# A four-layer graph transformer on one core: norm by groups between the keys, routed results kept by partition, and the output copied within DRAM

## The chip, the core and the metric

One core of one Trainium2 chip runs the whole network in one launch. The metric is the device time in microseconds (us) of an execution. The core has a matrix engine (TensorE, PE), a vector engine (VectorE, DVE), an engine for activations (ScalarE, ACT), a general engine (GpSimd, POOL) and a queue engine (SyncE, SP). SP, ACT and POOL each issue DMAs; 16 DMA engines carry them out.

## What is computed

3125 nodes with 256 features each pass through four layers. Every layer adds a graph attention over 103,125 edges and a global mixing of the normalised features to `x`, and then a feed-forward part:

```python
xn = _layernorm(x, axis=-1)
x = x + _L1_gnn_ref(xn, ..., src, dst) + _L1_mix_ref(xn[None], ...)[0]
x = x + _L1_ffn_ref(_layernorm(x, axis=-1)[None], ...)[0]
```

The mixing of layers 1 and 2 is linear attention: keys and values of all nodes are multiplied into one 32x32 matrix per head, then every query is multiplied with it. The feed-forward parts of layers 0 and 3 are routed: a softmax over eight experts picks two experts per node in layer 0 and one in layer 3, and the expert's result is weighted by its probability. In layer 3:

```python
H = gelu(xf @ W1 + b1); probs = softmax(H @ Wg + bg); assign = argmax(probs)
out = out + where(assign == e, probs[:, e:e+1] * (H @ Wd[e] + bd[e]), 0.0)   # for each e
```

## The kernel before

All node data stay on chip in tiles of 125 nodes, 25 of them: `x` and `xn` are 125 partitions x 25 x 256, and `xT` is the transposed norm. `GROUPS` cuts the 25 tiles into seven groups of 4, 4, 4, 4, 3, 3, 3. `begin_layer` norms all groups (`layernorm`: statistics on DVE, root on ACT, `xn` on DVE) and transposes them on PE (`transposed`). Most instructions are placed on their engine by a scheduler; inside a `manual_schedule` PE and DVE keep the written order. Work that can fill gaps is a Python generator, advanced by `next(work)`.

The stages, in the order of time:

- Layer 0: counts of edges, global mixing, graph attention with dense tiles, then `routed0`. Its results are scattered by an indirect DMA to `y_d` in DRAM, node by node, in two halves for the two experts; `route` works out which row each place is sent to. At the end both halves are read back in groups as (t p) f, one 1 KB piece per node, by SP (into `xn`) and ACT (into `xT`), and DVE adds them to `x`, weighted.
- Layer 1: `begin_layer`, then `beside`, which starts the generator `node_pieces` (graph attention's products per node tile, in tiles of 128 nodes) and lets `mix1` advance it. `mix1` calls `keys_values`: for each tile a product `p_kvt`, the key by ACT and DVE, the value by ACT, and the sum `p_kv`. Then come queries (`message`) and `network`, which adds `xn` and the bias `b2` to `x` on POOL. After that dense attention, a second attention (`dense_one`), and `ffn1`.
- Layer 2: `begin_layer`, the same with `mix2`, whose first instruction is the addition of `bproj` to all of `x` on POOL. Then dense attention and `ffn2`.
- Layer 3: `edge_attention` runs over the edges in 101 steps of 8 columns. In each, POOL gathers 8 x 128 rows `z_edge` by indirect DMA, DVE and ACT weight them (`near_e`), and PE sums them (`p_acc`). Once all tiles of a group are summed, the generator `hidden3` of that group runs piece by piece between the steps: norm, transposes, product with W1 (`p_h`, 8 parts of 128), Gelu on ACT, the router's scores, softmax, `first_max`, and rows of the hidden layer written to `hid_d` in DRAM through the tile `hid_row` (two buffers). `share` holds each node's probability.
- `routed3`: eight loads of `w_d`, alternately on ACT and SP, one of `bd`, `route`, and then for 32 tiles of 128 places a gather of `hid_tile` from `hid_d`, eight transposes (`p_t`), the product with the chosen expert (`p_q`), the bias, and a scatter to `y_d`. At the end, groups of `y_own` are read from `y_d`, multiplied by `share`, added to `x` and stored:

```python
y = w.tile([TP, 4, C], F32, name="y_own", bufs=4)
(nc.scalar if i % 2 else nc.sync).dma_start(y[:, :nt, :], y_d[t0 * TP:(t0 + nt) * TP, :].rearrange("(t p) f -> p t f", p=TP))
...
(nc.sync if i % 2 else nc.scalar).dma_start(out[:, t0:t0 + nt, :], x[:, t0:t0 + nt, :])
```

Of the kernel before, what the change touches and what calls it, by code (L numbers as in the profile page):

```python
# [42 lines left out]
PIECES0 = 101  # L43
# [3 lines left out]

GROUPS = [(0, 4), (4, 4), (8, 4), (12, 4), (16, 3), (19, 3), (22, 3)]
# [6 lines left out]
class Net:  # L55
# [811 lines left out]
    def keys_values(self, c, w, xT, wkv, work):  # L867
# [4 lines left out]
        with tc.tile_pool(name="la1", bufs=1, space=PSUM) as ps1, tc.tile_pool(name="la4", bufs=5, space=PSUM) as ps:  # L872
            p_kv = [ps1.tile([P, P + 1], F32, name=f"p_kv{m}") for m in range(KC)]
            for t in range(NT):
                ts = slice(t * TP, (t + 1) * TP)
# [9 lines left out]
                next(work, None)  # L885
# [23 lines left out]
    def mix1(self, x, xn, xT, work=iter(())):  # L909
        nc, tc = self.nc, self.tc  # L910
        with ExitStack() as s:
            c = s.enter_context(tc.tile_pool(name="m1", bufs=1))
            wkv = c.tile([P, KC, 2 * C], F32, name="wkv")
            for i, n in enumerate("kv"):
                nc.sync.dma_start(wkv[:, :, i * C:(i + 1) * C], self.ins["L1_mix_W" + n].rearrange("(k p) f -> p k f", p=P))
# [12 lines left out]
            with tc.tile_pool(name="m1k", bufs=2) as wk:  # L928
                kv, den = self.keys_values(c, wk, xT, wkv, work)
# [15 lines left out]
            def network(t0, nt):  # L945
# [24 lines left out]
                nc.gpsimd.tensor_add(xs, xs, xn[:, t0:t0 + nt, :])  # L970
                nc.gpsimd.tensor_add(xs, xs, b2[:, None, :].to_broadcast([TP, nt, C]))
# [108 lines left out]
    def mix2(self, x, xT, work=iter(())):  # L1080
        nc, tc = self.nc, self.tc
        with ExitStack() as s:
# [9 lines left out]

            nc.gpsimd.tensor_add(x, x, bproj[:, None, :].to_broadcast([TP, NT, C]))
            kv, den = self.keys_values(c, w, xT, wkv, work)
# [86 lines left out]
    def mix3(self, w, ps, x, xn, xT, weights):  # L1181
# [7 lines left out]
        zero = w.tile([P, 512], F32, name="hid_row", bufs=2)[:1, :KC * (P + 1)]  # L1189
# [3 lines left out]
        for t0, nt in GROUPS:  # L1193
# [9 lines left out]
            sq = w.tile([P, 8, 512], F32, name="h")[:TP, :2, :].rearrange("p a (b c) -> p (a b) c", c=C)[:, :nt, :]  # L1203
# [16 lines left out]
        s = w.tile([P, 512], F32, name="hid_row", bufs=2)[:, :KC * (P + 1)].rearrange("p (m f) -> p m f", m=KC)  # L1220
        nc.vector.tensor_copy(s, p_kv)
        yield
        kv = w.tile([P, 512], F32, name="hid_row", bufs=2)[:, :C].rearrange("p (m f) -> p m f", m=KC)
# [83 lines left out]
class Dense(Net):  # L1307
# [284 lines left out]
    def node_pieces(self, nodes, name, xT, H, slope, w, ps):  # L1592


        nc = self.nc
# [4 lines left out]
        yield  # L1600
# [7 lines left out]
        yield  # L1608
        es = w.tile([P, NS, H], F32, name="es")
        nc.gpsimd.memset(es[:, NS - 1, :], 0.0)  # L1610
        nc.gpsimd.memset(zs[:, NS - 1, :], 0.0)
# [412 lines left out]
    def route(self, c, one, nj):  # L2024

        nc, tc = self.nc, self.tc  # L2030
        _, T, E = one.shape
        node = c.tile([P, nj], I32, name="node_of")
# [547 lines left out]
```

## Time and profile before

| what | value |
|---|---|
| median of 10 runs | 5737.75 us (5728.58 to 5747.85) |
| profiled execution, and its span | 5742.5 us, 5740.6 us |
| mean granted clock of PE | 0.921 |
| edge attention of layer 3 | about 4400 to 5470 us of the span |
| from there to the first product of `routed3` | 5470 to 5540 us |
| products of `routed3` | 5540 to 5682 us |
| output | 5682 to 5741 us |

The profile is one execution, taken on the chip. PE is TensorE's products, PEld its loading of weights, which overlaps them. A line like "L709 PE MATMUL p_q<-w_d,hid_t" is one group of instructions: line of the code, engine, operation, what is written from what, then shapes, count, busy time and mean duration in ns, and what ended the idle time before it. L709 is the line of the helper `mm`, which issues nearly all products, so groups are told apart by their tiles. Line numbers in the prediction are those of the kernel before.

### The profile page before, as it was taken

What the parts mean: (1) busy time and instruction counts of PE and PEld (TensorE: products, weight loads), DVE (VectorE), ACT (ScalarE), POOL (GpSimd) and SP (SyncE); (2) the same over time, 40 slices, a digit from 0 to 9 for tenths busy, and PEclk for the clock granted to TensorE, in tenths of its full rate; (3) what the DMA queues carried; (4) which work ended last, traced back from release to release, by engine and by line L of the source; (5) the groups of instructions that cost most, each with busy time, mean ns of one, the idle gap of its engine ahead of it and who ended that gap; (6) DMA issues with size and microseconds to landing.
All of it is one profiled execution on the core that took longest, in us unless ns stands there. A gap on an engine that the chain in (4) does not pass through costs nothing.

```text
span 5740.6 us, 66349 instructions
## 1 busy us (share of the span) xinstructions
PE 4921.9 (86%) x24784; PEld 2863.3 (50%) x24784; DVE 3757.2 (65%) x5968; ACT 1022.6 (18%) x1932; POOL 1066.1 (19%) x1195
## 2 busy tenths in 40 slices
PE   3977888879578899989999899979997888898865
PEld 1652234448544433368645433345565555555555
DVE  6779999975445599845443899932223887777722
ACT  1540010011022200110123000022332112232210
POOL 1000000004220000000001100000002777777722
PEclk7989999979889999999889899989998889999978
DMA  2452222232200011111000011110002665666643
GB/s 84 34 38 87 76 64 66 67 113 64 88 16 0 23 34 35 33 42 36 22 1 4 26 33 39 30 58 1 0 1 79 155 159 158 178 171 169 168 157 123
DMA packets 299086, 391.54 MB, mean 68 GB/s; under 512 B 118746, under 2 KB 235583, under 8 KB 298249
## 3 DMA queue, kind: packets, MB, share of 16 engines
q1 hardware_dynamic: 204752, 160.01, 11.8%
q0 software_dynamic: 52336, 162.38, 10.7%
q10 hardware_dynamic: 41670, 64.82, 3.4%
q8 instruction: 202, 3.31, 0.3%
q14 instruction: 126, 1.03, 0.1%
HBM read 340.93 MB, written 46.13 MB: 67 GB/s over the span
## 4 chain that ended last, share of the span: by engine, by line
PE 39%; DVE 6%; DMA 5%; POOL 3%; issue 2%; ACT 1%; SPq 0%; DVEq 0%; ACTq 0%; POOLq 0%
PE p_tr L709 8%; PE p_acc L1976 5%; PE acc L1804 5%; PE p_y L709 5%; PE acc L1753 4%; POOL z_edge L1908 3%; DMA z_edge<-tab,src_i 2%; PE acc L1758 2%; PE p_h L709 2%; PE p_q L709 2%; DVE z_edge L1967 1%; DVE pt L1653 1%; PE p_kvt L709 1%; DVE zinv L1090 1%; DMA y_own<-y_d 1%
## 5 line engine op out<-in xcount | busy, mean ns | idle before, releaser
L1653 DVE SCALAR_TENSOR_TENSOR pt<-q_head,bar,a 128x750 f32<-128x750 f32 (+5 forms) x1200 | 1483.6, 1300 | 77.9 <-PE acc L1758 57.1
L1908 POOL DMA_INDIRECT z_edge<-tab,src_i x806 | 776.0, 963 | 271.9 <-issue 209.6
L1702 PE MATMUL acc<-pt,zs 128*64 128x500 f32 (+2 forms) x2800 | 594.0, 551 | 145.8 <-DVE pt L1653 145.4
L1753 PE MATMUL acc<-pt,zs 128*64 128x375 f32 (+2 forms) x3200 | 605.5, 501 | 18.3 <-DVE pt L1653 18.0
L1976 PE MATMUL p_acc<-z_edge,oh 128*125 128x264 f32 x2044 | 544.5, 428 | 88.6 <-DVE z_edge L1967 88.6
L1976 PEld LDWEIGHTS p_acc<-z_edge,oh 128*125 128x125 f32 x2044 | 423.8, 211 | 194.5 <-DVE z_edge L1967 98.2
L1702 PEld LDWEIGHTS acc<-pt,zs 128*64 128x64 f32 (+1 forms) x2800 | 246.0, 137 | 478.0 <-DVE pt L1653 321.7
L1753 PEld LDWEIGHTS acc<-pt,zs 128*64 128x64 f32 (+1 forms) x3200 | 243.5, 136 | 357.0 <-issue 217.3
L1171 DVE SCALAR_TENSOR_TENSOR x<-p_y,sm,x 125x256 f32<-125x256 f32 x200 | 93.9, 484 | 427.9 <-PE p_y L709 427.9
L1758 PE MATMUL acc<-pt,zs 128*32 128x375 f32 (+2 forms) x3200 | 313.4, 497 | 0.0
L1804 PE MATMUL acc<-zs,pt 128*125 128x257 f32 x1250 | 275.2, 383 | 11.9 <-DMA a<-count_d 11.9
L1804 PEld LDWEIGHTS acc<-zs,pt 128*125 128x125 f32 x1250 | 234.4, 188 | 52.7 <-issue 14.7
L1967 DVE TENSOR_TENSOR z_edge<-z_edge,near_e 128x2112 f32<-128x2112 f32 (+1 forms) x101 | 236.5, 2342 | 18.9 <-ACT near_e L1959 18.9
L1166 ACT ACTIVATE h<-p_tr,bn 128x500 f32<-128x500 f32 (+1 forms) x224 | 161.6, 722 | 361.9 <-PE p_tr L709 361.9
L286 PE MATMUL p_tr<-ident,xn 125*128 125x125 f32 x350 | 71.0, 355 | 165.0 <-DVE xn L612 138.3
L709 PE MATMUL p_y<-w_L_ffn_Wo,h 128*125 128x256 f32 x800 | 203.7, 387 | 0.0
L1653 DVE SCALAR_TENSOR_TENSOR pt<-q_all,bar,a 128x500 f32<-128x500 f32 (+3 forms) x175 | 119.1, 683 | 122.4 <-PE acc L1804 119.8
L709 PE MATMUL p_tr<-h,w_L_ffn_W 128*128 128x500 f32 (+1 forms) x448 | 192.1, 552 | 6.4 <-ACT h L1166 3.2
L1610 POOL MEMSET es<- 128x4 f32 (+2 forms) x4 | 1.3, 334 | 1050.0 <-PE acc L1758 721.3
L709 PE MATMUL p_tr<-xT,w_L_ffn_W 128*128 128x500 f32 (+1 forms) x448 | 194.8, 558 | 0.0
L2281 POOL CAST one_e<-one 125x96 bf16<-125x96 f32 (+1 forms) x2 | 2.1, 1050 | 1029.6 <-PE acc L1702 645.8
L1758 PEld LDWEIGHTS acc<-pt,zs 128*32 128x32 f32 (+1 forms) x3200 | 85.0, 109 | 202.8 <-issue 201.5
(496 smaller groups left out, 7093.1 us busy)
## 6 DMA issues: line engine op xcount, KB each, us to landing
row<-dst_row SPq DMA_DIRECT2D x101, 250.0 KB
a<-count_d SPq DMA_DIRECT2D x96, 203.1 KB
a<-count_d SPq DMA_DIRECT2D x96, 187.5 KB
a<-count_d SPq DMA_DIRECT2D x144, 93.8 KB
ef<-in_edge_s SPq DMA_DIRECT2D x101, 128.0 KB
z_edge<-tab,src_i POOLq DMA_INDIRECT x806
hid_d<-hid_row ACTq DMA_DIRECT2D x50, 250.0 KB
count_d<-stage SPq DMA_DIRECT2D x12, 781.2 KB
```

Source lines behind the costliest of these rows:

```text
L286: nc.tensor.transpose(p[:, t, :], src[:, t0 + t, k * P:(k + 1) * P], self.ident[:TP, :TP])
L709: self.nc.tensor.matmul(p, a, b, start=(i == 0), stop=(i == len(pairs) - 1))
L1166: nc.scalar.activation(o[:, m, :n], p[:, :n], AF.Relu, bias=b[:, e, m:m + 1], scale=g[:, e, m:m + 1])
L1171: nc.vector.scalar_tensor_tensor(x[:, t0 + t, :], q, wf[:, t, e:e + 1], x[:, t0 + t, :], op0=OP.mult, op1=OP.add)
L1653: self.nc.vector.scalar_tensor_tensor(pt[:K, :n], q, bar, a[:K, :n], op0=OP.max, op1=OP.mult)
L1702: nc.tensor.matmul(acc[64 * i:64 * i + 64, :b1 - b0], zs[:K, t, z:z + 64], pts[i][:K, b0:b1], start=(t == 0), stop=(t == NS - 1))
L1753: nc.tensor.matmul(acc[i // 2][64 * (i % 2):64 * (i % 2) + 64, b, :b1 - b0], zs[:K, t, i * W:i * W + 64], pts[i][:K, b0:b1], **st)
L1758: nc.tensor.matmul(acc[2][32 * i:32 * i + 32, b, :b1 - b0], zs[:K, t, z:z + 32], pts[i][:K, b0:b1], **st)
L1804: nc.tensor.matmul(acc[i], pt[:K, i * TP:(i + 1) * TP], zs[:K, t, :C + 1], start=(t == 0), stop=(t == NS - 1))
L1908: nc.gpsimd.indirect_dma_start(out=zs[i][:, j, :], out_offset=None, in_=table, in_offset=bass.IndirectOffsetOnAxis(ap=src[:, c0 + j:c0 + j ...
L1967: nc.vector.tensor_mul(zh, zh, weight[:, :, :, None].to_broadcast([P, n, H, D + 1]))
L1976: nc.tensor.matmul(acc[t], ohs[i, t][:, k - a, :], zs[i][:, k - c0, :HW], start=(k == cols[t][0]), stop=(k == cols[t][1] - 1))
```

## The change

- `begin_layer` before layers 1 and 2 goes. `keys_values` norms two groups first, then transposes each group when its first tile is due and norms the group after the next one. `node_pieces` works group by group and yields how many tiles of `xT` its next piece needs; `keys_values` advances it only when that many are there. `network` adds `xn` and `b2` on DVE, not on POOL. In `mix2` the addition of `bproj` stands after `keys_values`. `wkv` of layer 1 is loaded by POOL's queue.
- Layer 0's routed results and `xn_d` are stored by partition, (p t) f, so that a group's read is one piece of up to 4 KB for each partition; `route` computes the places accordingly.
- Layer 3: `hidden3` runs over `ENDS`, seven groups of three tiles and two of two. A row of `hid_d` has 1281 elements: the hidden row, the share and the node's `x`, which SP's queue writes straight from `x`. `hid_row` has four buffers. In `routed3` the gather brings all three, DVE finishes the row in its tile (share times result plus `x`) before the scatter, SP loads all of `w_d`, and the output is two copies from `y_d` to `out` within DRAM, on SP and ACT.

The diff, cut to its core:

```diff
@@ -40,11 +40,13 @@
 KEYS = HI * GN
-PIECES0 = 101
+PIECES0 = 107
 ...
 MARGIN = 4
+HID = 1024
+ENDS = [(0, 3), (3, 3), (6, 3), (9, 3), (12, 3), (15, 3), (18, 3), (21, 2), (23, 2)]
@@ -864,14 +866,26 @@
-    def keys_values(self, c, w, xT, wkv, work):
+    def keys_values(self, c, w, x, xn, xT, wkv, work):
 ...
         den = c.tile([P, KC, P], F32, name="kden")
-        with tc.tile_pool(name="la1", bufs=1, space=PSUM) as ps1, tc.tile_pool(name="la4", bufs=5, space=PSUM) as ps:
+        with tc.tile_pool(name="la1", bufs=1, space=PSUM) as ps1, tc.tile_pool(name="la4", bufs=3, space=PSUM) as ps, \
+                tc.tile_pool(name="lat", bufs=2, space=PSUM) as pst:
             p_kv = [ps1.tile([P, P + 1], F32, name=f"p_kv{m}") for m in range(KC)]
+            self.layernorm(xn, x, GROUPS[0])
+            self.layernorm(xn, x, GROUPS[1])
+            need, done = 0, 0
+            begins = {g[0]: i for i, g in enumerate(GROUPS)}
             for t in range(NT):
+                if t in begins:
+                    i = begins[t]
+                    self.transposed(pst, xT, xn, groups=[GROUPS[i]])
+                    done = sum(GROUPS[i])
+                    if 0 < i < len(GROUPS) - 1:
+                        self.layernorm(xn, x, GROUPS[i + 1])
@@ -882,7 +896,8 @@
                     nc.tensor.matmul(p_kv[m], key[:, m * P:(m + 1) * P], v[:, m, :], start=(t == 0), stop=(t == NT - 1))
-                next(work, None)
+                if t > 1 and need <= min(done, NT):
+                    need = next(work, 0)
@@ -912,7 +927,7 @@
             for i, n in enumerate("kv"):
-                nc.sync.dma_start(wkv[:, :, i * C:(i + 1) * C], self.ins["L1_mix_W" + n].rearrange("(k p) f -> p k f", p=P))
+                nc.gpsimd.dma_start(wkv[:, :, i * C:(i + 1) * C], self.ins["L1_mix_W" + n].rearrange("(k p) f -> p k f", p=P))
@@ -967,8 +982,8 @@
                 nc.vector.tensor_mul(o, o, g2[:, None, :].to_broadcast([TP, nt, C]))
-                nc.gpsimd.tensor_add(xs, xs, xn[:, t0:t0 + nt, :])
-                nc.gpsimd.tensor_add(xs, xs, b2[:, None, :].to_broadcast([TP, nt, C]))
+                nc.vector.tensor_add(xs, xs, xn[:, t0:t0 + nt, :])
+                nc.vector.tensor_add(xs, xs, b2[:, None, :].to_broadcast([TP, nt, C]))
@@ -1090,8 +1105,8 @@
                 nc.vector.tensor_mul(out, num, z)
+            kv, den = self.keys_values(c, w, x, xn, xT, wkv, work)
             nc.gpsimd.tensor_add(x, x, bproj[:, None, :].to_broadcast([TP, NT, C]))
-            kv, den = self.keys_values(c, w, xT, wkv, work)
@@ -1592,12 +1607,18 @@
         gw = self.gnn_weight(w, ps, name, H, "p_a")
-        yield
+        es = w.tile([P, NS, H], F32, name="es")
 ...
+        yield GROUPS[0][1]
+        at = 0
@@ -1605,19 +1626,16 @@
             nc.sync.dma_start(q_d[:, cs], q)
-        yield
-        es = w.tile([P, NS, H], F32, name="es")
 ...
-        for t in range(NS):
 ...
-            yield
+            yield t0 + nt
+            while at < NS and min((at + 1) * P, N) <= (t0 + nt) * TP:
+                t, at = at, at + 1
 ...
+                yield t0 + nt + (4 if at < NS and min((at + 1) * P, N) > (t0 + nt) * TP else 0)
@@ -1986,7 +2003,7 @@
                         nc.vector.tensor_add(x[:, t, :], x[:, t, :], o.rearrange("p h d -> p (h d)"))
-                        for t0, nt in GROUPS:
+                        for t0, nt in ENDS:
@@ -2048,7 +2066,7 @@
             spare = w.tile([P, nj], F32, name="spare")
-            nc.gpsimd.iota(spare, pattern=[[P, nj]], base=T * TP + 1, channel_multiplier=1, allow_small_or_imprecise_dtypes=True)
+            nc.gpsimd.iota(spare, pattern=[[P, nj]], base=T * TP + (T == NT), channel_multiplier=1, allow_small_or_imprecise_dtypes=True)
@@ -2109,17 +2127,22 @@
             code = w.tile([P, nj], F32, name="code")
-            nc.vector.scalar_tensor_tensor(code, p_n[:, 1], float(TP), n_1, op0=OP.mult, op1=OP.add)
             at_n = w.tile([P, nj], F32, name="at_n")
-            nc.vector.tensor_scalar(at_n, code, -1.0, 0.0, op0=OP.add, op1=OP.max)
             if T > NT:
+                nc.vector.scalar_tensor_tensor(code, n_1, float(NT), p_n[:, 1], op0=OP.mult, op1=OP.add)
+                nc.vector.tensor_scalar(at_n, code, -float(NT), 0.0, op0=OP.add, op1=OP.max)
                 over_n = w.tile([P, nj], F32, name="over_n")
-                nc.vector.tensor_scalar(over_n, at_n, float(N), -float(N), op0=OP.is_ge, op1=OP.mult)
-                nc.vector.tensor_add(node, at_n, over_n)
+                nc.vector.tensor_scalar(over_n, p_n[:, 1], float(NT), float(NT), op0=OP.is_ge, op1=OP.mult)
+                nc.vector.tensor_sub(node, at_n, over_n)
+                nc.vector.scalar_tensor_tensor(at_n, over_n, float(N // NT - 1), at_n, op0=OP.mult, op1=OP.add)
+                nc.vector.scalar_tensor_tensor(spare, code, 0.0, spare, op0=OP.is_equal, op1=OP.mult)
+                nc.vector.tensor_add(to, at_n, spare)
 ...
@@ -2153,15 +2177,16 @@
             yield
-        h = w.tile([P, F, 512], F32, name="h")
+        h = w.tile([P, F, 3 * TP], F32, name="h")
 ...
             nc.scalar.activation(h[:, f, :n], p[:, :n], AF.Gelu, bias=b1[:, f:f + 1], scale=1.0)
-            yield
+            if f % 2:
+                yield
 ...
         self.mm(p[:E, :n], [(wg[:, f, :], h[:, f, :n]) for f in range(F)])
-        sc = w.tile([P, 512], F32, name="hid_row", bufs=2)[:E]
+        sc = w.tile([P, 513], F32, name="hid_row", bufs=4)[:E]
@@ -2173,39 +2198,44 @@
         nc.vector.tensor_mul(one, one, prob)
-        nc.vector.tensor_reduce(share[:, t0:t0 + nt], one, AX.X, OP.add)
+        share = w.tile([TP, 4], F32, name="share")
+        nc.vector.tensor_reduce(share[:, :nt], one, AX.X, OP.add)
+        nc.sync.dma_start(hid_d[t0 * TP:(t0 + nt) * TP, HID + 1:].rearrange("(t p) f -> p t f", p=TP), x[:, t0:t0 + nt, :])
 ...
                     nc.tensor.transpose(p[:TP, f * P:(f + 1) * P], h[:, 4 * i + f, t * TP:(t + 1) * TP], self.ident)
-                row = w.tile([P, 512], F32, name="hid_row", bufs=2)[:TP]
-                nc.scalar.activation(row, p[:TP], AF.Copy)
-                nc.scalar.dma_start(hid_d[(t0 + t) * TP:(t0 + t + 1) * TP, i * 512:(i + 1) * 512], row)
+                row = w.tile([P, 513], F32, name="hid_row", bufs=4)[:TP]
+                nc.scalar.activation(row[:, :512], p[:TP], AF.Copy)
+                if i:
+                    nc.scalar.activation(row[:, 512:], share[:, t:t + 1], AF.Copy)
+                nc.scalar.dma_start(hid_d[(t0 + t) * TP:(t0 + t + 1) * TP, i * 512:(i + 1) * 512 + i], row[:, :512 + i])
                 yield
-    def routed3(self, x, ones, share, hid_d, out):
+    def routed3(self, ones, hid_d, out):
         nc, tc = self.nc, self.tc
-        E, F, HID = 8, 8, 1024
+        E, F = 8, 8
 ...
             for e in range(E):
-                (nc.sync if e % 2 else nc.scalar).dma_start(wd[:, :, e, :], self.ins["L3_ffn_Wd"][e].rearrange("(k p) f -> p k f", p=P))
+                nc.sync.dma_start(wd[:, :, e, :], self.ins["L3_ffn_Wd"][e].rearrange("(k p) f -> p k f", p=P))
 ...
             ps = s.enter_context(tc.tile_pool(name="r3q", bufs=2, space=PSUM))
-            mat, hts = {}, {}
+            mat, hts, hrs = {}, {}, {}
             def rows(j):
-                hr = w.tile([P, HID], F32, name="hid_tile")
+                hr = hrs[j] = w.tile([P, HID + 1 + C], F32, name="hid_tile", bufs=4)
@@ -2224,6 +2254,7 @@
                 nc.vector.tensor_add(y, q, bd[:, bass.ds(mat[j], C)])
+                nc.vector.scalar_tensor_tensor(y, y, hrs[j][:, HID:HID + 1], hrs[j][:, HID + 1:], op0=OP.mult, op1=OP.add)
@@ -2232,13 +2263,10 @@
                         products(j - 1)
-            for i, (t0, nt) in enumerate(GROUPS):
-                y = w.tile([TP, 4, C], F32, name="y_own", bufs=4)
-                (nc.scalar if i % 2 else nc.sync).dma_start(y[:, :nt, :], y_d[t0 * TP:(t0 + nt) * TP, :].rearrange("(t p) f -> p t f", p=TP))
-                for t in range(nt):
-                    nc.vector.scalar_tensor_tensor(x[:, t0 + t, :], y[:, t, :], share[:, t0 + t:t0 + t + 1], x[:, t0 + t, :],
-                                                   op0=OP.mult, op1=OP.add)
-                (nc.sync if i % 2 else nc.scalar).dma_start(out[:, t0:t0 + nt, :], x[:, t0:t0 + nt, :])
+            for i, q in enumerate((nc.sync, nc.scalar)):
+                a, b = i * 62 * 25, 62 * 25 if i == 0 else N
+                q.dma_start(out[a:b, :].rearrange("(p t) f -> p (t f)", t=25), y_d[a:b, :].rearrange("(p t) f -> p (t f)", t=25))
@@ -2264,7 +2292,7 @@
                     self.layernorm_twice(xn, x, (a, na))
-                    nc.sync.dma_start(xn_d[a * TP:(a + na) * TP, :].rearrange("(t p) f -> p t f", p=TP), xn[:, a:a + na, :])
+                    nc.sync.dma_start(xn_d.rearrange("(p t) f -> p t f", p=TP)[:, a:a + na, :], xn[:, a:a + na, :])
@@ -2367,8 +2395,8 @@
                 for i, y in enumerate((xn[:, t0:t0 + nt, :], back)):
-                    a = i * N + t0 * TP
-                    (nc.scalar if i else nc.sync).dma_start(y, y_d[a:a + nt * TP, :].rearrange("(t p) f -> p t f", p=TP))
+                    own = y_d[i * N:(i + 1) * N, :].rearrange("(p t) f -> p t f", p=TP)
+                    (nc.scalar if i else nc.sync).dma_start(y, own[:, t0:t0 + nt, :])
@@ -2416,7 +2444,6 @@
                 self.routed0(x, xn, xT, xn_d, gate, self.routed0_weights(wp))
-        self.begin_layer(x, xn, xT)
@@ -2427,16 +2454,14 @@
             self.ffn1(x, xn, xT, weights)
-        self.begin_layer(x, xn, xT)
 ...
             gw = self.gnn2_weights(ap)
-            nodes = self.beside(ap, "g2", xT, 4, 0.2, lambda work: self.mix2(x, xT, work))
+            nodes = self.beside(ap, "g2", xT, 4, 0.2, lambda work: self.mix2(x, xn, xT, work))
 ...
             ones = lp.tile([TP, NT, 8], BF16, name="one_e")
-            share = lp.tile([TP, NT], F32, name="share")
-            hid_d = self.dram.tile([N, 1024], F32, name="hid_d")
+            hid_d = self.dram.tile([N, HID + 1 + C], F32, name="hid_d")
@@ -2447,8 +2472,8 @@
                     x, xT, edge, lambda w, ps: self.mix3(w, ps, x, xn, xT, mix),
-                    lambda w, ps, t0, nt: self.hidden3(w, ps, x, xn, xT, t0, nt, hid, ones, share, hid_d))
-            self.routed3(x, ones, share, hid_d, out)
+                    lambda w, ps, t0, nt: self.hidden3(w, ps, x, xn, xT, t0, nt, hid, ones, hid_d))
+            self.routed3(ones, hid_d, out)
```

## The prediction

> **What bounds the kernel now.** I read the page first, then a table of stages made from windows of the span, then the chain of waits in the tail, and last the transfer rates, the groups and the timeline of the stages that the change touches. The page says that TensorE (PE) is busy for most of the span and carries most of the chain that ended last. It cannot say which stages leave it idle, and that is what the change is about.
>
> ```profile
> PE 4921.9 (86%) x24784; PEld 2863.3 (50%) x24784; DVE 3757.2 (65%) x5968; ACT 1022.6 (18%) x1932; POOL 1066.1 (19%) x1195
> PE 39%; DVE 6%; DMA 5%; POOL 3%; issue 2%; ACT 1%; SPq 0%; DVEq 0%; ACTq 0%; POOLq 0%
> ```
>
> The table of stages (window, its length, busy time and count of PE, weight loads, DVE, ACT and POOL, then granted clock, DMA share, GB/s) has four stretches in which PE is nearly idle or waits: 1521 to 1588 (read-back after layer 0's routed part), 1588 to 1628 (norm before layer 1), 5497 to 5540 (before the last products) and 5682 to the end.
>
> ```profile
> 1521.00:1588.00 67.00, 0.00 (x0) 0.00 (x0) 20.30 (x50) 1.28 (x1) 0.97 (x3) 0.51 0.46 145
> 1588.00:1628.00 40.00, 13.97 (x53) 9.64 (x54) 38.24 (x90) 5.66 (x14) 30.83 (x18) 0.50 0.02 6
> 1628.00:1720.00 92.00, 91.58 (x333) 51.02 (x333) 15.44 (x54) 36.44 (x107) 2.24 (x22) 0.98 0.01 1
> 3048.00:3056.00 8.00, 7.32 (x50) 6.85 (x50) 6.09 (x15) 3.77 (x8) 5.06 (x2) 0.79 0.14 49
> 3056.00:3152.00 96.00, 91.46 (x334) 50.65 (x335) 19.55 (x53) 36.44 (x107) 11.66 (x25) 0.98 0.00 1
> ...
> 5497.00:5540.00 43.00, 11.18 (x59) 9.35 (x57) 12.15 (x49) 3.58 (x6) 4.06 (x5) 0.50 0.81 284
> 5540.00:5682.00 142.00, 138.74 (x752) 123.24 (x752) 34.63 (x63) 17.95 (x30) 58.57 (x60) 0.99 0.44 138
> 5682.00:5741.00 59.00, 0.00 (x0) 0.00 (x0) 10.34 (x25) 0.00 (x0) 0.00 (x0) 0.52 0.31 109
> ```
>
> The chain of waits (start, length, what) shows what the tail waits for: rows of `hid_d` written twice in a row, then a load, a gather, the products, and the reading of `y_d`.
>
> ```profile
> 5475.14 17.40 PE p_h L709 x48
> ...
> 5496.93 13.04 DMA hid_d<-hid_row
> 5510.68 10.93 DMA hid_d<-hid_row
> 5523.06 7.07 DMA m_L_ffn_bd<-in_L_ffn_bd
> 5530.12 5.11 DMA hid_tile<-hid_d,node_of
> 5535.64 3.91 PE p_t L2215 x16
> 5540.41 5.41 PE p_q L709 x16
> ...
> 5682.88 19.89 DMA y_own<-y_d
> ```
>
> Two strips of GB/s in 40 slices: 5680 to 5741, where everything moves in rows of 125 partitions, and 5497 to 5535, where the 128-partition weights `w_d` move first.
>
> ```profile
> GB/s 38 59 32 97 121 121 121 121 121 121 121 121 121 121 121 121 121 121 120 121 121 121 121 121 120 121 121 121 120 121 124 111 120 121 119 115 121 107 24 0
> GB/s 382 380 384 385 323 356 381 390 392 389 390 388 391 384 389 386 264 355 388 301 128 123 125 125 126 119 122 120 213 315 391 413 397 398 215 161 181 241 362 319
> ```
>
> A 125-row transfer holds 121 GB/s at a DMA share of about 0.3 (the last stage's row), which is five of 16 engines at 24 GB/s each; the weights get 390 from all 16.
>
> **Part 1, output.** Removed: seven loads of `y_own`, 25 DVE multiply-adds and seven stores, which are 6.4 MB at 121 GB/s = 53 us of the 58 from 5682.3 (the last scatter's landing) to the end. Added: one multiply-add per tile on DVE ahead of the scatter (0.48 us, the row of the same operation in the final stage). The products repeat every 4.33 us with PE busy 138.7 of 142, while DVE does 34.6 of 142 and would do 50: hidden on all tiles but the last, so +0.5. The gather's row grows from 4096 to 5124 bytes: 656 KB in 4.33 us is 152 GB/s, below 390, hidden by the prefetch of four tiles; if that cover were gone, a 5.1 us gather instead of 4.33 would cost 0.8 on 32 tiles, 25 us. Then two copies within DRAM, in 32 rows each, 3.2 MB. No such copy is in the trace. At best it moves like the weights, 3.2 MB / 390 = 8.2 us; if reading and writing the same memory halve that rate, 16.4; on five engines, 26.5. Both ends of it are DRAM, unlike the row of the weights, so I take 16.4. With 0.5, 0.6 us to start (5682.3 to 5682.9), a landing of 2.4 (the last scatter's) and about 2 from the last bytes to the end of the span, the stage is 22 and the gain **36** (26 to 45). The Trainium skill, "DMA: Bandwidth & Descriptors", section "Latency and other measured facts", gives copies between HBM tensors a full rate of 207 to 214 GB/s per direction. No run here shows that yet; as an estimate from that page, 3.2 / 0.21 = 15 us, where the weights' row alone would give 8.
>
> **Part 2, the last group.** The last group has two tiles of nodes instead of three. Its `p_h` products, 17.4 us for 375 columns, become 17.4 x 250/375 = 11.6: 5.8 earlier. `hid_row` has four buffers for two: the last group needs one for the scores and four for rows, so the waits of 13.0 and 10.9 us for a buffer mostly go. What is late next is the transfers: 8.4 MB of `w_d`, all on SP's queue behind the last write of `x` rows, which only needs the finished rows; 1 MB of `bd` and 1 MB of rows on ACT's. In before the weights start at 5493.9, just after the last read of `bg` (5493.6); with 5.8 less, 5488. 10.4 MB / 390 = 27 us: 5515 at the latest if the rows share evenly, then gather 5.1, transposes and first product 5.3 (5530.1 to 5540.4 in the chain): 5525, or 5520 if the rows land ahead of the weights. Against 5540.4 I take **18** (8 to 28; the low end is rows that wait behind all of `w_d`). The routing's own DVE work, 12.2 us in the stage's row, is done before that.
>
> **Part 3, edge attention, where the other groups are finished.** Nine groups for seven, the same columns, pieces of two products. The built order has 78 activation table loads between the first and the last `near_e` where before has 74, at 1.28 us each, beside an ACT engine that is mostly idle. Writing `x` beside the rows adds 3.2 MB of 125-row transfers, 26 us of five engines over 1070 us. On the other side, ACT waited 35.5 us for `hid_row`. POOL sets the pace: 806 gathers at 0.96 us and 0.26 of issue between them are 982 of 1070 us. I take **0** (25 either way, from those two figures).
>
> **Part 4, norm by groups in layer 1.** In this stage DVE is the bound, and slowed:
>
> ```profile
> L612 DVE TENSOR_SCALAR xn<-x,mv,rstd 125x256 f32<-125x256 f32 x25 | 24.1, 1025 | 0.0
> L970 POOL TENSOR_TENSOR x<-x,xn 125x1024 f32<-125x1024 f32 (+1 forms) x7 | 14.9, 2128 | 8.2 <-DVE xn L612 8.2
> ```
>
> `xn` takes 1.03 us on average beside POOL's additions, while its median is 0.41. After the change two groups (8 tiles) come first: 8 x (0.40 + 0.16 + 0.41) and 0.8 for the roots is 8.5, eight transposes at 0.43 and a copy of 0.6 are 4: keys start at 1600.5 instead of 1628.3, 27.8 saved. Back come the other 42 transposes on a PE that is full there (91.6 of 92): 42 x 7.32/50 = 6. DVE gets 17 more norms (16.4), 14 additions that were POOL's (the nearest row, a 125x1024 product of two tensors, is 1.08: 13.5 in all), nine keys at 0.42 and the copies of `xT`: some 37 us that the built order puts before the tenth key, against 9 x 3.7 = 33 of PE. I charge 5 for it. POOL no longer works beside DVE, so I keep 0.41 for `xn`. The pieces of the node products go on later, in about the same amount. `wkv` moves to POOL's queue, behind nothing but small fills. Net **17** (3 to 25).
>
> **Part 5, the small ones.** Layer 0's read-back keeps 125 rows and so five engines; only its pieces grow from 1 to 4 KB. Loads with 8 KB pieces hold 391 to 413 and with 1 KB 380 to 390, 3% of 55 us: **2** (0 to 5). Before layer 2 the norm was already hidden behind layer 1's last part, and the removed stretch is 8 us with PE busy 7.3; its transposes go into a key loop that had 4.5 us of idle PE: **3**. The addition of `bproj` on POOL (13.7 us) stays next to the first keys, which it slowed before too; one more key slowed as then (4.7 us for 0.42) would cost 4, two 8: -6 to 8.
>
> **Sum.** 36 + 18 + 0 + 17 + 2 + 3 = 76. The profiled execution took 5742.5 with a span of 5740.6, so it becomes 5666.5 and 5664.6; it is 4.75 above the median 5737.75 of the runs, which becomes 5661.75, rounded to 5662. About 0.2%, 11.5 us, can be told from no change.
>
> **Rivals.** (A) The transfers stay slow: the copy runs on five engines (26.5 us, stage 32, gain 26), `w_d` on one queue ends near 5520 (gain 10), DVE holds the keys (gain 5). With 2 + 3 that is 46: 5692. For it: every transfer of node rows in the trace runs at 121. Against: 32 rows divide among 16 engines as the 128 of the weights do. Chance 0.17. (B) The copy moves like the weights, 8 us, and the edge stage gains half of ACT's 35 us of waits: 76 + 8 + 17 = 101, 5637. Chance 0.2. (C) Slower: rows of 5124 bytes do not start on round addresses. If each such write took twice as long, `hid_d`'s 12.8 MB would cost 106 us more on its five engines and the 3.2 MB of `x` 53: 159 us in the edge stage, 5737.75 - 76 + 159 = 5821. It decides from 87 us, if over half of it reaches the end. For it: the gathers share those engines, and DVE waits 84 us for `z_edge`. Against: the DMA share there is 0.61 to 0.65 and POOL, not the transfers, keeps the pace. Chance 0.07. (D) Parts give back what others gain, within 11.5 us: 0.03. The sum above keeps 0.53. The Trainium skill, same page, section "How a descriptor splits into AXI transactions", says that a piece that starts off a 256-byte boundary costs one more transaction; by that, an estimate, a 2 KB piece costs one in eight more, not double, and 12.8 MB 13 us of five engines instead of 106.
>
> A, B and the sum are all faster: 0.90. The range of 8 in 10 leaves out C, D and the far ends of A and B: 5628 (gain 110) to 5697 (gain 41).
>
> **What would show it.** Right: no `y_own`, and 15 to 25 us from the last scatter to the end, with over 180 GB/s in that strip; first `p_q` 15 to 20 us nearer to the last `p_acc`, with no wait of ACT for `hid_row` above 5 us; first `p_kvt` of layer 1 about 12 us after layer 0's last addition and no `xn` of 1 us. Wrong: an output strip at 121, `p_q` waiting for `w_d`, keys with gaps that end at DVE, or an edge stage whose 101 steps take longer than 1070 us.

## The result, and the profile after

The changed kernel takes 5649.44 us (median of 8 runs, 5637.51 to 5663.87) against 5738.38 us for the kernel before (28 runs). The ratio is 0.9844 with a 95% interval from 0.9836 to 0.9853: 1.6% faster, 89 us. The forecast was 5662 us, with a range from 5628 to 5697. The profiled execution took 5650.21 us with a span of 5648.1.

```profile
PE 4903.2 (87%) x24880; PEld 2859.6 (51%) x24880; DVE 3783.6 (67%) x6022; ACT 1041.2 (18%) x1993; POOL 1037.2 (18%) x1183
PE 25%; DVE 6%; issue 4%; POOL 4%; DMA 3%; ACT 1%; DVEq 0%; ACTq 0%; POOLq 0%; SPq 0%
```

The second line gives the shares of the chain that ended last, by engine. PE's share of the span went from 86 to 87%, with 4903.2 us busy instead of 4921.9: about the same work, and less standing still. The table of windows of the changed kernel, with the columns of the prediction's table, has the stretches that were idle before:

```profile
1573.00:1580.00 7.00, 3.86 (x16) 3.21 (x16) 6.28 (x31) 0.87 (x3) 1.17 (x4) 0.50 0.00 1
1580.00:1670.00 90.00, 88.06 (x333) 48.80 (x333) 44.08 (x121) 45.04 (x116) 2.23 (x22) 0.97 0.00 1
...
5429.00:5492.00 63.00, 24.00 (x118) 17.58 (x116) 17.28 (x70) 12.00 (x24) 6.50 (x10) 0.65 0.63 219
5492.00:5632.00 140.00, 139.07 (x752) 123.49 (x752) 49.73 (x94) 17.92 (x30) 57.84 (x59) 0.98 0.50 162
5632.00:5649.00 17.00, 0.00 (x0) 0.00 (x0) 0.05 (x1) 0.00 (x0) 0.97 (x1) 0.62 0.59 200
```

To see where 92.5 us of span went, I took from both traces the first or last start of one instruction that bounds each stage. "Again" is a second profile of the kernel before, from the experiments; it shows which differences come between two profiles of one kernel.

| from, to | before | again | after | gain (before to after) | forecast |
|---|---|---|---|---|---|
| start, first dense product of layer 0 | 438.6 | 439.3 | 422.9 | 15.7 | not costed |
| to layer 0's first scatter | 860.6 | 862.0 | 861.4 | -0.8 | 0 |
| to layer 0's last addition (with the read-back) | 288.4 | 288.2 | 288.4 | 0 | 2 |
| to the first key of layer 1 | 40.7 | 40.0 | 7.7 | 33.0 | 27.8 |
| to the last key | 88.7 | 89.8 | 86.8 | 1.9 | -11 |
| to the dense part of layer 1 | 269.7 | 264.5 | 271.4 | -1.7 | 0 |
| to the first key of layer 2 | 1069.8 | 1069.4 | 1066.1 | 3.7 | 3, with the next row |
| to the last key | 92.7 | 92.7 | 98.0 | -5.3 | in the row above |
| to the end of layer 2's dense part | 567.1 | 567.2 | 565.4 | 1.7 | 0 |
| to the first `p_acc` of layer 3 | 715.6 | 706.7 | 708.0 | 7.6 | 0 |
| edge stage, first to last `p_acc` | 1037.1 | 1039.0 | 1053.3 | -16.2 | 0 |
| tail, last `p_acc` to first `p_q` | 71.4 | 71.2 | 62.5 | 8.9 | 18 |
| products | 138.4 | 138.5 | 138.8 | -0.4 | 0 |
| last product to the end | 61.8 | 61.7 | 17.4 | 44.4 | 36 |

The 7.6 us ahead of layer 3 are not the change's: the second profile of the kernel before has them too (706.7).

The tail and the output of the changed kernel in its timeline (start, length, engine, operation, and in brackets the idle time before it):

```profile
5448.02 34.89 SPq L2229 DMA_DIRECT2D w_d<-in_L_ffn_Wd x8
5454.02 0.29 ACTq L2214 DMA_DIRECT2D hid_d<-hid_row  x1
5469.64 1.04 POOL L2239 DMA_INDIRECT hid_tile<-hid_d,node_of  x1 [35.57 <-DMA hid_d<-hid_row]
5491.94 5.80 PE L711 MATMUL p_q<-w_d,hid_t 128*128 x16 [10.81 <-DMA w_d<-in_L_ffn_Wd]
...
5632.33 0.97 POOL L2406 DMA_INDIRECT y_d<-y_tile,to_row  x1 [2.48 <-DVE y_tile L2257]
5634.88 0.57 SPq L2269 DMA_DIRECT2D out<-y_d  x1
5634.88 0.62 ACTq L2269 DMA_DIRECT2D out<-y_d  x1
```

The last rows are issued at 5454.0 without a wait for a buffer, the first gather waits for them until 5469.6, and the first `p_q` for `w_d` until 5491.9. The copies start at 5634.9, and 13.2 us later the span is over.

### The profile page after: what moved, and what is told of

It is laid out like the page before. It is cut to its first block, busy times and chain, and to the rows that moved or that the text cites. A ratio compares the mean times of both kernels' runs of the same rounds, so it can differ in the third digit from the quotient of the medians.

```text
span 5648.1 us, 66627 instructions
## 1 busy us (share of the span) xinstructions
PE 4903.2 (87%) x24880; PEld 2859.6 (51%) x24880; DVE 3783.6 (67%) x6022; ACT 1041.2 (18%) x1993; POOL 1037.2 (18%) x1183
## 5 line engine op out<-in xcount | busy, mean ns | idle before, releaser
L711 PEld LDWEIGHTS p_y<-w_L_ffn_Wo,h 128*125 128x125 f32 x800 | 145.0, 187 | 73.4 <-ACT h L1181 27.1
```

The costliest lines, as they stand in the source:

```text
L711: self.nc.tensor.matmul(p, a, b, start=(i == 0), stop=(i == len(pairs) - 1))
```

## The experiments

Every experiment is an edit of the changed kernel, timed beside the kernel before on the same chip, so the ratios to before can be compared. The chips differ: before took 5730 to 5736 us beside `wd_two`, `late_scores`, `groups7`, `aligned`, `before_again`, `yield_each` and `x_late`, but 6023 to 6028 beside `norm_first_1`, `adds_pool`, `pieces_101`, `copy_125` and `spread`. In the profiles of the second kind all stages but the edge stage have their usual times, and only those are used from them. One stretch varies on both kinds and with no edit that touches it: from the first dense product of layer 0 to its first scatter, `late_scores`, `aligned`, `yield_each` and `copy_125` took 873.4 to 874.4 us, all others 859.6 to 863.9. So stages are compared here, not the spans of single profiles.

**Layer 1: norm by groups, or additions off POOL?** First the norm put back ahead of the keys (`normed` then also leaves out the transposes in `keys_values`), then the additions put back on POOL.

```diff
+        self.begin_layer(x, xn, xT)
         with tc.tile_pool(name="da", bufs=1) as c, tc.tile_pool(name="elu", bufs=2) as w:
...
-            self.layernorm(xn, x, GROUPS[0])
-            self.layernorm(xn, x, GROUPS[1])
...
+            if not normed:
+                self.layernorm(xn, x, GROUPS[0])
+                self.layernorm(xn, x, GROUPS[1])
```

> The changed kernel with begin_layer put back before layer 1: all norms and transposes of layer 1 ahead of the keys, the additions on DVE kept. Theory 1 (the norm by groups is worth what the stage showed, 40 us from layer 0's last addition to the first key before the change, 7 after): the first key comes 24 to 34 us after that addition (less than 40, since POOL adds nothing beside it and xn stays at 0.41 us), the keys take 83 to 90 us instead of 89.4, and the kernel is 18 to 30 us slower than the changed one. Theory 2 (the contention with POOL was the real cost, not the order): the first key comes within 15 us and the kernel loses less than 8 us.

```diff
-                nc.vector.tensor_add(xs, xs, xn[:, t0:t0 + nt, :])
-                nc.vector.tensor_add(xs, xs, b2[:, None, :].to_broadcast([TP, nt, C]))
+                nc.gpsimd.tensor_add(xs, xs, xn[:, t0:t0 + nt, :])
+                nc.gpsimd.tensor_add(xs, xs, b2[:, None, :].to_broadcast([TP, nt, C]))
```

> The changed kernel with the two additions of network back on POOL. Theory 1 (POOL's additions slow DVE's norms, which are now beside the keys): xn goes from 0.41 us to near 1, the key loop of layer 1 grows from 89.4 us by 5 to 20 us, and the kernel loses 5 to 20 us. Theory 2 (beside a PE that sets the pace of the keys the slower norms do not matter): xn gets slower, but the key loop stays within 3 us and the kernel within 4 us of the changed one.

| | last addition to first key | first to last key | both |
|---|---|---|---|
| before | 40.7 | 88.7 | 129.4 |
| norm by groups, additions on POOL (`adds_pool`) | 7.7 | 102.7 | 110.4 |
| norm first, additions on DVE (`norm_first_1`) | 24.4 | 77.9 | 102.3 |
| both (changed kernel) | 7.7 | 86.8 | 94.5 |

The ratios, 0.9837 [0.9800, 0.9874] and 0.9877 [0.9847, 0.9907], are too wide for effects of this size; the stages decide. `norm_first_1`: its first number holds (24.4 us, in the range of theory 1), but the key loop gives back 8.9 us, because the norms and transposes are out of it, so on top of the moved additions the norm by groups is worth 7.8 us, not 18 to 30. `adds_pool`: theory 1, the key loop is 15.9 us longer. The groups of DVE instructions in `adds_pool` and then in the changed kernel, window from layer 0's last additions to the queries:

```profile
L614 DVE TENSOR_SCALAR xn<-x,mv,rstd 125x256 f32<-125x256 f32 x25 | 19.1, 820 | 0.1
L721 DVE SCALAR_TENSOR_TENSOR key<-elu_ek,elu_rk 125x256 f32<-125x256 f32 x25 | 17.6, 705 | 43.9 <-ACT elu_rk L720 43.8
```

```profile
L721 DVE SCALAR_TENSOR_TENSOR key<-elu_ek,elu_rk 125x256 f32<-125x256 f32 x25 | 10.6, 423 | 39.1 <-ACT elu_rk L720 39.0
L614 DVE TENSOR_SCALAR xn<-x,mv,rstd 125x256 f32<-125x256 f32 x25 | 8.8, 406 | 0.0
```

Beside POOL's additions a norm takes 0.82 us instead of 0.41 and a key 0.71 instead of 0.42. The Trainium skill, "SBUF — State Buffer", section "Who interferes with whom", says why such pairs collide: GpSimd and VectorE share a pair of ports, which VectorE uses for instructions with two inputs in SBUF and in its two-port modes, and the later of two such instructions is blocked until the earlier one is over. The rows agree: a single `xn` of `adds_pool` took up to 2.50 us, as long as one addition of 125x1024 on POOL (2.34 to 2.44).

**Layer 0: what moved its start?**

```diff
-PIECES0 = 107
+PIECES0 = 101
```

> The changed kernel with PIECES0 at 101, the value of before, node_pieces by group kept. The last count tile of layer 0 was stored at 398.6 us where before had 418.7, and the dense products of layer 0 start at 422.9 instead of 438.6. Theory 1 (the number of pieces ahead of the counts is what moved them): the dense products start 10 to 16 us later again and the kernel loses that much. Theory 2 (the group-wise order of node_pieces, with its products spread between the counts, is what did it): they start at 420 to 428 as in the changed kernel, within 5 us.

The dense products start at 419.5 us, in the changed kernel and the other experiments at 417.6 to 422.9, in the kernel before at 438.6. The constant does nothing. Theory 2 is left, the order of `node_pieces`: its first product in layer 0 runs at 337.4 us instead of 366.4, and the other edit in layer 0 ahead of its scatter, the storing of `xn_d`, first runs at 798. That order was not undone by itself. The ratio, 0.9836 [0.9803, 0.9868], is too wide to add to this.

**Output: are rows what spreads a copy?**

```diff
-                a, b = i * 62 * 25, 62 * 25 if i == 0 else N
-                q.dma_start(out[a:b, :].rearrange("(p t) f -> p (t f)", t=25), y_d[a:b, :].rearrange("(p t) f -> p (t f)", t=25))
+            for q, a, b in ((nc.sync, 0, 12), (nc.scalar, 12, 25)):
+                q.dma_start(out.rearrange("(p t) f -> p (t f)", t=25)[:, a * C:b * C], y_d[:N, :].rearrange("(p t) f -> p (t f)", t=25)[:, a * C:b * C])
```

> The changed kernel with the output copied in 125 rows: 12 of the 25 tiles' columns on SP and 13 on ACT, each row a piece of 12 or 13 KB, instead of 62 and 63 runs of 50 KB cut in 32 rows. The end took 13.5 us from the last scatter's landing to the end of the span. Theory 1 (125 rows run on five engines): 3.2 MB at 121 GB/s are 26.5 us, the end takes 30 to 34 us and the kernel loses 17 to 21. Theory 2 (a copy within DRAM is spread by its pieces, not by its rows): 13 to 16 us, loss under 4.

From the last product to the end it takes 32.9 us instead of 17.4. The strips from 5918 to 5950 us (busy share of the 16 DMA engines in tenths, and GB/s) stand at the rate of five engines:

```profile
DMA  0022003333332323323323323323323233331000
GB/s 0 20 87 77 10 10 77 123 138 129 137 138 111 160 111 129 155 111 137 143 114 145 145 110 143 143 114 145 145 127 143 127 129 147 131 133 67 33 0 0
```

Theory 1 holds for copies within DRAM as for loads: 125 rows cost 15.5 us more than 32. The 250 pieces of this copy take 25.5 us, 126 GB/s. In the changed kernel's trace they are 64 pieces, 32 of 49,600 and 32 of 50,400 bytes, and take 10.1 us, 317 GB/s. (Its 62 and 63 rows in the code have 25.6 KB each; the 50 KB of the expectation are these pieces.) The ratio to before, 0.9844 [0.9815, 0.9873], cannot show 15 us.

**Tail: what does the first `p_q` wait for?**

```diff
-                nc.sync.dma_start(wd[:, :, e, :], self.ins["L3_ffn_Wd"][e].rearrange("(k p) f -> p k f", p=P))
+                (nc.sync if e % 2 else nc.scalar).dma_start(wd[:, :, e, :], self.ins["L3_ffn_Wd"][e].rearrange("(k p) f -> p k f", p=P))
```

> The changed kernel with w_d loaded alternately on ACT and SP, as before the change; everything else is kept. Theory 1 (one queue cannot keep the engines fed: in the changed kernel SP needs 34.9 us to issue the eight loads and the strip of GB/s dips to between 126 and 180 for some 6 us): the dip goes, the first p_q comes 52 to 56 us after the last p_acc instead of 62.5, and the kernel gets 6 to 10 us faster. Theory 2 (rows of hid_d that sit behind weights on ACT's queue are what holds the gathers): ACT's four loads stand ahead of the last rows again, the rows land later than 5469.6 - 5429.4 = 40 us after the last p_acc, and the first p_q comes no earlier, 62 to 72 us after it. Theory 3 (the sum of bytes decides): 13.1 MB move either way, no change within 3 us.

The tail is 61.9 us instead of 62.5, although the last rows are issued 33 us after the last `p_acc` instead of 25: theory 3, neither the queue nor the order of the rows. That what moves before the first `p_q` decides is also what `x_late` below shows, where 3.2 MB more make the tail 14.1 us longer. Ratio 0.9859 [0.9833, 0.9884].

**Edge stage: why is it 9 to 16 us longer?** Five edits. The first takes away DVE's wait for the scores, the second aligns the rows, the third brings seven groups back (with two buffers of `hid_row`), the fourth takes the writes of `x` out of the stage, the fifth stops after every product again, as before the change.

```diff
             nc.tensor.transpose(p[:TP, t * E:(t + 1) * E], sc[:, t * TP:(t + 1) * TP], self.ident[:E, :E])
+        yield
```

> The changed kernel with one more yield in hidden3, between the transposes of the scores on PE and the first DVE instruction that reads them. Edge attention took 1037 us from the first to the last p_acc before the change and 1053 after it. Theory 1 (DVE, which runs in written order, stands still until PE gets to the transposes of the scores; its waits for p_h there grew from 25.4 us in five to 41.5 us in eight): those waits fall below 10 us and the stage is 15 to 30 us shorter. Theory 2 (the transfers of the longer rows slow the gathers): the waits go but the stage stays within 5 us of 1053. Theory 3 (the loss is the count of activation table loads): no change, the same 95 or so.

```diff
-            hid_d = self.dram.tile([N, HID + 1 + C], F32, name="hid_d")
+            hid_d = self.dram.tile([N, HID + 64 + C], F32, name="hid_d")
...
-                    nc.scalar.activation(row[:, 512:], share[:, t:t + 1], AF.Copy)
+                    nc.scalar.activation(row[:, 512:], share[:, t:t + 1].to_broadcast([TP, 64]), AF.Copy)
```

> The changed kernel with rows of hid_d padded to 1344 elements (5376 bytes, a multiple of 256): the share fills 64 elements, and x starts at element 1088. So every piece starts on a multiple of 256 bytes; the bytes grow by 5%. Theory 1 (pieces off a 256-byte boundary slow the edge stage): the stage falls from 1053 us towards 1037, and the DVE wait for z_edge falls below 79 us. Theory 2 (alignment is not what matters): the stage stays within 6 us of 1053, and the tail within 3 us of 62.5.

```diff
-ENDS = [(0, 3), (3, 3), (6, 3), (9, 3), (12, 3), (15, 3), (18, 3), (21, 2), (23, 2)]
+ENDS = GROUPS = [(0, 4), (4, 4), (8, 4), (12, 4), (16, 3), (19, 3), (22, 3)]
```

> The changed kernel with the seven groups of four and three tiles in layer 3 again (h 512 wide, and hid_row with two buffers, which is what fits beside it); rows with share and x, the copy and the rest are kept. Theory 1 (nine groups instead of seven cost the edge stage fixed waits): the stage from the first to the last p_acc comes back from 1053 to about 1037 us. Theory 2 (the rows with x and share do it): it stays at 1050 or more. Either way the tail loses: three tiles in the last group and two buffers make the first p_q come 68 to 80 us after the last p_acc instead of 62.5, so the whole is between 10 us faster and 15 us slower than the changed kernel.

```diff
-        nc.sync.dma_start(hid_d[t0 * TP:(t0 + nt) * TP, HID + 1:].rearrange("(t p) f -> p t f", p=TP), x[:, t0:t0 + nt, :])
...
+            nc.sync.dma_start(hid_d[:, HID + 1:].rearrange("(t p) f -> p t f", p=TP), x)
             wd = c.tile([P, F, E, C], F32, name="w_d")
```

> The changed kernel with all rows of x written to hid_d by one DMA ahead of the loads of w_d, instead of group by group between the steps. Theory 1 (these writes, or SP's queue that carries them, slow the edge stage): it is 8 to 16 us shorter than that of the changed kernel. Theory 2 (pieces of two products do it): within 4 us. Either way the tail has 3.2 MB more in 125-row pieces ahead of the weights, at 121 GB/s 26 us if nothing shared the engines: the first p_q 66 to 85 us after the last p_acc instead of 62, and the whole 0 to 20 us slower.

```diff
-            if f % 2:
-                yield
+            yield
```

> The changed kernel with hidden3 stopping after every product p_h again instead of after every second one. Theory 1 (pieces of two products are too long for the gaps of a step, since PE then comes late to p_acc and POOL's gathers wait for it, 45 us in the late steps instead of 25): the edge stage is 8 to 16 us shorter than that of the changed kernel on the same chip, near the one of before. Theory 2 (the rows of x and share do it): within 4 us of the changed kernel's, 1048 to 1053 on a chip like the first.

The kernel before was profiled again:

> The kernel before once more, unchanged: a second look at its edge stage, which the comparison rests on. The first look had 1037.1 us from the first to the last p_acc; four kernels with the changed edge stage had 1047.9 to 1053.3, one with seven groups 1058.0. Theory 1 (the changed stage is truly longer): 1033 to 1041. Theory 2 (one look of this stage spreads by more than 10 us): 1045 or more, and there is no loss to explain.

The last column but one is what POOL waits in all, over the edge stage, for the `p_acc` products that free its `z_edge` buffers.

| | edge stage | tail | both | POOL's wait | ratio to before |
|---|---|---|---|---|---|
| before, again | 1037.1, 1039.0 | 71.4, 71.2 | 1108.5, 1110.2 | 28.6, 28.0 | 1.0001 [0.9991, 1.0011] |
| changed | 1053.3 | 62.5 | 1115.8 | 50.4 | 0.9844 [0.9836, 0.9853] |
| `wd_two` (same edge stage) | 1048.3 | 61.9 | 1110.2 | 46.8 | 0.9859 [0.9833, 0.9884] |
| `late_scores` | 1047.9 | 62.1 | 1110.0 | 40.9 | 0.9850 [0.9829, 0.9872] |
| `aligned` | 1048.1 | 62.8 | 1110.9 | 49.7 | 0.9851 [0.9834, 0.9867] |
| `groups7` | 1058.0 | 71.2 | 1129.2 | 57.9 | 0.9900 [0.9883, 0.9916] |
| `x_late` | 1051.8 | 76.6 | 1128.4 | 49.6 | 0.9876 [0.9860, 0.9893] |
| `yield_each` | 1021.8 | 79.3 | 1101.1 | 16.0 | 0.9826 [0.9810, 0.9842] |

The loss is real: two profiles of before agree within 2 us, and two of the changed stage, 1053.3 and 1048.3, lie 9 to 16 above them. `late_scores` took the waits for the scores away altogether, and the stage did not get shorter than that of `wd_two`: the waits only moved, and the idle time of PE that ends at DVE's `z_edge` ahead of `p_acc` grew from 206.6 to 232.4 us. Alignment, the writes of `x` and the count of groups are not the cause either; `groups7` and `x_late` show instead what the smaller last group and the four buffers are worth together (the tail is 71.2 us again without them) and what 3.2 MB more in the tail cost (14 us). Only `yield_each` shortens the stage. POOL's waits show how, in before, the changed kernel and `yield_each`, each over its edge stage (total, times, longest):

```profile
POOL z_edge L1908 <- PE p_acc L1976: 28.6, 30, 5.3
```

```profile
POOL z_edge L1925 <- PE p_acc L1993: 50.4, 37, 5.1
```

```profile
POOL z_edge L1925 <- PE p_acc L1993: 16.0, 29, 5.1
```

A piece of two products keeps PE from `p_acc` for longer, and the gathers, which set the pace, wait for it. The stage follows this wait over all nine profiles: from `yield_each` to `groups7`, whose pieces are two products of up to 500 columns, the wait grows by 41.9 us and the stage by 36.2. But not all of the 31 us is gain: with smaller pieces the last group but one is not done when the stage ends, and two groups of products fall into the tail, 64 MATMUL records of `p_h` with W1 instead of 32. That leaves 324 of them in the stage instead of 356, 9% fewer, while POOL's wait falls to a third, so the moved group alone does not explain the shorter stage. Over stage and tail it is 9 to 15 us better than the changed kernel; the intervals of the two ratios overlap, so that the whole kernel is faster is likely and not shown. I tried to clear the pile with a third call of `piece()` in every fourth step:

```diff
                         targets(i + 1)
+                    if i % 4 == 3:
+                        piece()
```

> The kernel that stops hidden3 after every product (yield_each), with a third call of piece() in every fourth step of the edge stage, so that the smaller pieces do not pile up. With yield_each the stage was 1021.8 us, but two groups of rows were left for the tail, 79.3 us to the first p_q instead of 62.5: 1101 together, against 1108 to 1110 before the change and 1110 to 1116 after it. Theory 1 (the length of a piece is what costs, not the number of pieces): one group is left for the tail, which is 61 to 64 us again, the stage takes 1022 to 1036, and the kernel is 10 to 25 us faster than the changed one, ratio to before 0.980 to 0.983. Theory 2 (what is done between the steps costs the same however it is cut): the tail gets shorter by 17 us and the stage longer by as much, ratio 0.982 to 0.9845.

It ran on a chip of the second kind: ratio 0.9904 [0.9883, 0.9925], edge stage 1379.8 us where other kernels had 1327.3 to 1345.7 there, tail 64.5. One group was left for the tail, as expected, but neither theory foresaw a longer stage by 34 to 52 us, in which POOL's wait for `p_acc` is 322.8 us where the others there have 234 to 264. On that kind of chip the stage waits for something the profile does not name, so what the extra call does on the first kind is open, and no version is shown to beat the changed kernel.

## Why the prediction was right, and where its steps were not

The sum, 76 us, came close to the 89 measured in part by luck, since its errors cancel. The output brought 8.4 us more than forecast, the norm in layer 1 17.9 more, and layer 0's start 15.7 that no term had; the last group brought 9.1 less, the small terms 4.9 less, and the edge stage lost up to 16.2. Another 7.6 us between the two profiles are not the change's.

- **Output, 36 forecast, 44.4 measured.** Mechanism right, rate wrong. I halved the weights' rate because both ends are DRAM, and the rate of 207 to 214 GB/s agreed that the Trainium skill gives ("DMA: Bandwidth & Descriptors", section "Latency and other measured facts"). That rate was measured on another pattern, 16 KiB rows with a pitch, and does not hold for this one: 3.2 MB took 13.2 us with start and landing, at least 242 GB/s, and the pieces themselves run from 5636.2 to 5646.3 us, 10.1 us or 317 GB/s, against the weights' 390. The case I had set aside, 8.2 us, which is half of rival B, was the better one. The gather's longer rows and the operation on DVE were hidden as costed: the products took 138.8 us against 138.4.
- **Last group, 18 forecast, 8.9 measured.** The start of the weights came as costed: 18.6 us after the last `p_acc` instead of 24.9. The term that failed is the 27 us for 10.4 MB. Four gathers ahead, 2.6 MB, belong to it, and 13.1 MB moved in the window from 5440 to 5500, 34 us at 390 GB/s. Nor did the rate hold. In the strip there it falls to 126 in the middle:

```profile
GB/s 11 0 0 0 0 0 221 330 299 360 391 383 380 377 154 126 180 362 305 229 356 350 370 400 390 409 402 391 350 347 347 326 121 76 4 0 0 0 11 0
```

  The queues from 5462 to 5464 us (packets, MB, share of 16 engines) show ACT's rows of 125 partitions (q10) and SP's weights (q1) side by side, at a share of 0.33 together, about that of five engines:

```profile
q10 hardware_dynamic: 83, 0.17, 21.8%
q1 hardware_dynamic: 81, 0.08, 11.6%
```

  From the first weight to the first `p_q` it took 43.9 us, before 46.5, where the forecast had 32 to 37. So the waits of 13.0 and 10.9 us for a buffer went away as forecast, and the transfers behind them kept nearly the same end. `p_q` waiting for `w_d` was among the prediction's signs of being wrong. Rival A's gain of 10 for this part came near, but not for its reason: a second queue changed nothing (`wd_two`).
- **Edge stage, 0 forecast, 9 to 16 lost.** I costed table loads and bytes, and named the "pieces of two products" without a price. They were the cause: POOL waits 50.4 us instead of 28.6 for `p_acc`, and 16.0 with pieces of one product. Rival C's misaligned rows cost nothing that can be seen: aligned rows gave 1048.1 us for the stage against 1048.3 and 1053.3, and the transaction that the Trainium skill (same page, section "How a descriptor splits into AXI transactions") adds off a 256-byte boundary does not show here.
- **Norm in layer 1, 17 forecast, 34.9 measured to the last key.** The front part was near (27.8 forecast, 33.0 measured: the norms took 0.41 us, and the first key came 7.7 us after the last addition, not 12.5, since the first transposes started 0.5 us after the first `xn`, not behind all eight). Wrong were the two charges of 6 and 5: the key loop got 1.9 us shorter. The transposes did come in, but `node_pieces` waits for its groups and hands products on to the queries, where PE has gaps: its `p_a` products took 37.9 us of PE in the loop before and 27.5 after. I had written that these go on "in about the same amount". The experiments add that POOL's additions were the larger part of the problem: of the 34.9 us, moving them alone gives 27.1 (129.4 to 102.3) and the norm by groups alone 19.0 (129.4 to 110.4).
- **Layer 0's start, 15.7, was not in the sum.** I read `node_pieces` as layer 1's affair; it also runs between layer 0's counts.
- **Small ones, 2 and 3 forecast, 0 and 0.1 measured.** The read-back with 4 KB pieces took the same 288.4 us. In layer 2 the parts gave 3.7, -5.3 and 1.7. The key loop is 5.3 us longer because its first key stands beside the addition of `bproj` for longer: that key took 11.3 us instead of 4.7, and the sum behind it waits 9.6 us instead of 4.1. The forecast had a price for one more slowed key, not for the same key slowed more. The changed kernel's rows:

```profile
3006.31 13.67 POOL L1109 TENSOR_TENSOR x<-x,r_L_mix_bproj 125x6400 f32<-125x6400 f32 x1 [3.27 <-DVE xn L614]
3008.97 11.63 DVE L721 SCALAR_TENSOR_TENSOR key<-elu_ek,elu_rk 125x256 f32<-125x256 f32 x2 [2.74 <-ACT elu_rk L720]
3020.41 1.20 PE L898 MATMUL p_kv<-val,key 125*128 125x129 f32 x4 [9.60 <-DVE key L721]
```

## What to carry to other kernels

Before a move to a finer interleaving, price the pieces by the longest thing that one of them keeps waiting; here pieces of two products cost the stage more than any of its added transfers. Transfers in 125 rows moved 121 to 126 GB/s here, to and from the chip and within DRAM alike, and those in 128 or 32 rows 390 and 317, so data that only pass through are better laid out for a few long rows that spread over all engines. And an engine that looks free, like POOL, can be the wrong place for additions over whole tiles while DVE is on the path: beside them DVE's norms took twice as long.

## What the runs showed of the hardware

The same kernels ran at two speeds on different chips: 5730 to 5738 us and 6023 to 6028 for the kernel before. In the profiles of the second kind the other stages agree within their usual spread, and the edge stage alone takes 1327 to 1380 us instead of 1022 to 1058. Its largest wait (engine and line, total, times, longest; `spread`, edge stage) is put down to nothing on this core, which no wait of the edge stage is on the first kind:

```profile
ACT m_sb L1955 <- remote: 444.0, 31, 22.4
```

What ACT waits for there was not settled. On either kind the changed kernel's variants beat the kernel before.
